# A four-layer decoder on one core: keys and values of two cross attentions behind the expert tiles, expert rows fetched back block by block, VectorE kept in the order of the step table

## Chip, cores and metric

The kernel runs on one core of a Trainium2 chip. The metric is device time in microseconds (us) of one launch. Runs of one kernel differ by some tenths of a per cent, so a time is the median of several.

## What is computed

The input `x` is 32 sequences of 64 tokens with 128 features, and `ctx` is of the same shape. Four layers follow each other, and each has three parts, each with a residual and a layer norm behind it:

```
for each layer:   x = LN(x + attn(x));  x = LN(x + xattn(x, ctx));  x = LN(x + ffn(x))
layer 0: rope attention (16 heads of 8) | gated two-way cross attention | two local-window transformer layers
layer 1: latent attention (16 heads of 64) | cross attention | 8 experts, one per token, none dropped
layer 2: attention with alibi            | cross attention | 8 experts, one per token, at most 80 tokens each
layer 3: rope attention                  | cross attention with masks | linear layer with both sides rounded to fp8
```

What matters here is that the keys and values of a cross attention, `k = ctx Wk + bk` and `v = ctx Wv`, depend on `ctx` alone, and so on nothing that the layers before it compute. In the attention with alibi a number that grows with the distance between query and key is added to each score.

## The kernel before

The 2048 tokens are four blocks (`NBLK`) of 512 tokens, that is eight sequences or four tiles of 128 tokens. `Decoder` has a method for each part of a layer. Each method puts closures into a table, `Steps` (L259): `sp.at(step, place, f)` files `f` under a step and a place within it, and `run` calls all of them in the order of step and place. Steps of different parts interleave, so that one block's attention runs beside the next block's preparation. The order of PE's instructions is that of the table (`manual_schedule` for PE at the end of the program). The order of the other engines' instructions, and of the DMAs issued by SP and POOL, is chosen by a list scheduler when the program is built; each engine then works through its instructions strictly in that order.

An 8-wide attention (`attn8`, L630) has 16 scores, four per block. For block `blk` at base step `base`, `prepare` (L653) runs in three steps the k part, the q part and the v part of `attn8_prep` (L516): a projection on PE, a copy out of PSUM by ACT (for rope, two projections and two DVE operations), and for k the *wide* product `kx` (L561): two tiles of 128x1024, on POOL, where each key row is masked for four heads. `self.wide` is the last of these. The values go into `v8`, two constant tiles that alternate between blocks and hold a column of ones per head. `attn8_scores` (L580) puts masks or alibi into PSUM by bf16 matmuls with an identity, adds q times kx, and then DVE takes the maximum (`mx`, L610) and the difference (`p`), and ACT the exponential (L613). Two steps later `attn8_turn` transposes p on PE (`ptps`, L624) and ACT copies it (`pT`, L626); `values` multiplies with v (`o`). `turn_a`, `out` (y) and `normal_x` finish a half block; `turn_x` (L494) transposes the new x for the next part (`xTps`, `xT`). A norm (`norm`, L458) is bn_stats and bn_aggr on DVE, 1/sqrt by two operations on POOL (`rstd`, L419), and the scaling on ACT, DVE or POOL. Scores have two PSUM buffers, all else on PE shares four (`G`).

Alibi is kept as three bf16 parts. The high and middle parts lie on 128 partitions and go in by one matmul per head group; the low part is on 64 partitions and goes in by a second one.

The experts (`sorted_experts` L1321, `capacity_experts` L1461) work like this: `routed` (L1274) computes logits and choices block by block beside the cross attention and scatters each token's row to a DRAM buffer sorted by expert (POOL, indirect DMA). When all rows are there, tiles of up to 128 rows are loaded, multiplied by their expert's weights, and scattered back to `token_y` in DRAM. The weights of all eight experts lie in `wbig`, 128 partitions by eight times 1156 columns. The first expert stage copies a tile's weights out of `wbig` (L1383); the second reads them in place. `wbig` is refilled for the second by `fetch` (L1468), 24 loads on SP, as soon as the copies of the first are done. Then `rows_back` (L1438 and L1528) loads a block of rows: block 0's behind all scatters, and those of blocks 1 to 3 behind `self.wide` as well, all three from one place in the table. `added` adds the residual (or multiplies by the gate, L1535) and norms; `turn_x` follows. Meanwhile the next attention (l2a in layer 2, l3a in layer 3) starts with block 0.

Names of the parts: l1x, l2x, l3x are the cross attentions of layers 1 to 3, l2a and l3a the self attentions of layers 2 and 3, l1f and l2f the expert stages, l3f the fp8 layer. For l2a the base step is 96, for l2x 112, for l3a 137, for l3x 153.

`fp8_linear` (L1616) rounds the weights once (`weights`: load, ACT product `kh`, then eight DVE operations on `qe` and `em`), and for each block of x rounds it in four DVE pieces, multiplies, adds and norms.

Of the kernel before, what the change touches and what calls it, by code (L numbers as in the profile page):

```python
# [20 lines left out]
P = 128  # L21
# [73 lines left out]
def _alibi():  # L95
# [10 lines left out]
    low = (ali - hi.astype(f) - mid.astype(f)).astype(ml_dtypes.bfloat16)  # L106
    return np.concatenate([np.concatenate([hi, mid], 0), np.concatenate([low, low], 0)], 1)
# [151 lines left out]
class Steps:  # L259


    def __init__(self):
        self.work = {}
# [4 lines left out]
    def run(self):  # L268
        for key in sorted(self.work):
            for f in self.work[key]:  # L270
                f()


class Decoder:
# [66 lines left out]
    def setup(self):  # L341
# [48 lines left out]
        for n in range(2):  # L390
            v = self.const([P, BPB, 8, 2, 9], f"v8_{n}")
            nc.gpsimd.memset(v, 0.0)
            nc.gpsimd.memset(v[0:64, :, :, 0, 8:9], 1.0)
            nc.gpsimd.memset(v[64:128, :, :, 1, 8:9], 1.0)
            self.v8.append(v)

# [30 lines left out]
    def layernorm(self, z, last=False):  # L427
# [3 lines left out]
        for t in range(TPB):  # L431
            nc.vector.bn_stats(st[:, t, :], z[:, t, :])
            nc.vector.bn_aggr(mv[:, t, :], st[:, t, :])
# [24 lines left out]
    def norm(self, blk, z, pool=True, number=False, part=(0, TPB)):  # L458

# [5 lines left out]
        for t in range(n):  # L467
            nc.vector.bn_stats(st[:, t, :], z[:, t0 + t, :])
            nc.vector.bn_aggr(mv[:, t, :], st[:, t, :])  # L469
        r = self.rstd(mv[:, 0:n, 1], n)  # L470
        if t0 == 0:
            full = self.xfull[blk] = self.const([P, TPB, XR], "x", bufs=5)
            self.xt[blk], self.xT[blk] = full[:, :, 0:D], None
            if number:
                nc.gpsimd.tensor_copy(
                    full.bitcast(I32)[:, :, D:], bc(self.tokens[:, blk * TPB : (blk + 1) * TPB], 2, XR - D)
                )
        x = self.xt[blk]
# [15 lines left out]
    def turn_x(self, blk, part=(0, TPB)):  # L494
# [6 lines left out]
        self.nc.scalar.copy(self.xT[blk][:, t0 * P : (t0 + n) * P], ps[:, 0 : n * P])  # L501
# [14 lines left out]
    def attn8_prep(self, blk, w, src, rope, scale, bqs, quick):  # L516
# [23 lines left out]
        def q_part():  # L540
# [3 lines left out]
            elif "bq" in w:  # L544
                nc.scalar.activation(qT, proj("wq", self.xT[blk]), AF.Identity, bias=bqs, scale=scale)
            else:
                nc.scalar.mul(qT, proj("wq", self.xT[blk]), scale)

        def k_part():
            kT = self.q2([P, TB], "k8")  # L550
            if rope is not None:
                turned("wk", "bk", src(blk), rope[:, 128:256], kT)
            elif "bk" in w:
                nc.scalar.activation(kT, proj("wk", src(blk)), AF.Identity, bias=w["bk"], scale=1.0)  # L554
            else:
                nc.scalar.copy(kT, proj("wk", src(blk)))
# [8 lines left out]

        def v_part():
            x = src(blk)
# [5 lines left out]
            v = got["v"] = self.v8[blk % 2]  # L573
# [4 lines left out]
        return got, (k_part, q_part, v_part)  # L578

    def attn8_scores(self, blk, pp, gg, prep, mask):  # L580
# [5 lines left out]
        for h in range(2):  # L586
# [8 lines left out]
            elif kind == "heads":  # L595
                o2 = o.rearrange("p (n c) -> p n c", n=2)
                self.mm(o2, self.ident2, bc(m[:, g * 256 : (g + 1) * 256], 1, 2), True, False)
                self.mm(o2, self.ident2[0:64, :], bc(m[0:64, 1024 + g * 256 : 1024 + (g + 1) * 256], 1, 2), False, False)
# [31 lines left out]
    def attn8(self, sp, base, name, src=None, rope=None, scale=1.0, row=None, mask=(None, None), has_out=True, split=False, number=False, turned=None):  # L630
# [22 lines left out]
        def prepare(blk, i):  # L653
            if i == 0:
                prep[blk] = self.attn8_prep(blk, setup["w"], src, rope, scale, setup.get("bqs"), quick and blk == 0)
            prep[blk][1][i]()
# [80 lines left out]
        sp.at(base - 4, 3, start)  # L737
        for blk in range(NBLK):
            for i in range(3):
                sp.at(base + 4 * blk - 4 + i, 4, lambda blk=blk, i=i: prepare(blk, i))  # L740
# [460 lines left out]
    def route(self, lg, oh, gate=None):  # L1201
# [3 lines left out]
        mx = self.sb([P, TPB], "rmx", 4)[:, 0:n]  # L1205
        nc.vector.tensor_reduce(mx, lg, AX.X, ALU.max)
        if gate is not None:
            self.tt(lg, lg, bc(mx, 2, 8), ALU.subtract)
            nc.scalar.activation(lg, lg, AF.Exp)
# [64 lines left out]
    def routed(self, sp, st, ready, wr, br, base, rows, dst, bound, gated):  # L1274
# [10 lines left out]

        def choose(t0, n):
# [4 lines left out]
            self.route(st.pop(("lg", t0))[:, 0:n, :], st["oh"][:, t, :], st["gate"][:, t] if gated else None)  # L1291
# [479 lines left out]
```

## Time and profile before

| what | value |
|---|---|
| median of 5 runs | 1463.95 us (1458.01 to 1468.05) |
| the profiled execution | 1465.63 us, of which the span from first to last instruction is 1463.9 |
| PE busy | 1242.2 us, 85% of the span |
| DVE, ACT, POOL busy | 925.2, 688.8, 734.8 us |
| mean granted PE clock | 0.882 |
| the chain that ended last | PE 57%, DVE 16%, POOL 12%, ACT 8%, issue 4%, DMA 2% |

The page of the profile lists lines of `kernel.py` (L335 is the helper for all matmuls, L338 the helper for all tensor_tensor operations), so groups are told apart by the names of their tiles: `out<-in`. The windows view cuts the span into stretches that one chooses and gives each engine's busy time in each, the clock that PE was granted (1.00 is full speed), the share of the DMA engines and the GB/s that they moved. The chain of waits goes back from the last instruction, at each step to what released it, and is then listed in order of time: start, length, engine, tile and line. The timeline lists the instructions of an engine in order; for SP these are the DMAs that it issues, with the time at which they were issued. PE's busy time includes half-speed stretches: the same matmul takes longer there.

### The profile page before, as it was taken

The numbers are of one execution on the slowest core, as the hardware profiler recorded it, in microseconds if no ns is written. First come the engines' busy times: TensorE is split into PE (matmuls) and PEld (weight loads), VectorE is DVE, ScalarE is ACT, GpSimd is POOL, SyncE is SP. The second block draws the span as 40 slices with busy tenths as digits, with TensorE's granted clock in tenths as the row PEclk, the third lists the DMA queues.
The fourth block names the chain that finished last, engine by engine and source line by source line (L and its number), as shares of the span: only waits on it lengthen the run. The fifth ranks groups of instructions, "written<-read, shape, count | busy, mean of one in ns | idle before, by whom it ended". The sixth has DMA issues, their size and how long they took to land.

```text
span 1463.9 us, 36933 instructions
## 1 busy us (share of the span) xinstructions
PE 1242.2 (85%) x16009; PEld 898.7 (61%) x16009; DVE 925.2 (63%) x1819; ACT 688.8 (47%) x1174; POOL 734.8 (50%) x609
## 2 busy tenths in 40 slices
PE   7997888889887898989889995949999855899992
PEld 4775555556555555666567775916677753577772
DVE  6754577777786677657564655635677434667775
ACT  3453445555554544554545532634566311546642
POOL 3524688777785655445532443522445232444542
PEclk9998899999999999999999975968999557889955
DMA  6001010350010000100010002230000001000000
GB/s 231 2 2 24 0 45 2 127 163 2 1 53 1 1 1 2 54 14 2 2 34 35 2 17 62 73 118 2 2 9 5 3 12 36 2 1 2 3 9 22
DMA packets 33714, 43.16 MB, mean 29 GB/s; under 512 B 5946, under 2 KB 27121, under 8 KB 33168
## 3 DMA queue, kind: packets, MB, share of 16 engines
q1 hardware_dynamic: 31536, 38.20, 8.1%
q8 instruction: 126, 2.06, 0.6%
q0 software_dynamic: 2016, 2.60, 0.6%
q14 instruction: 36, 0.29, 0.1%
HBM read 26.63 MB, written 15.56 MB: 29 GB/s over the span
## 4 chain that ended last, share of the span: by engine, by line
PE 57%; DVE 16%; POOL 12%; ACT 8%; issue 4%; DMA 2%; SPq 0%; POOLq 0%; ACTq 0%; DVEq 0%
PE s L335 13%; PE o L335 9%; PE ptps L624 6%; PE qkps L335 5%; DVE turn L338 5%; PE proj L335 5%; POOL turn L338 4%; PE y L335 4%; PE ropeT L877 3%; ACT pT L626 2%; DVE rn L1037 2%; POOL rstd L338 2%; DVE p L338 2%; PE vps L335 2%; POOL rn L338 2%
## 5 line engine op out<-in xcount | busy, mean ns | idle before, releaser
L610 DVE TENSOR_REDUCE mx<-s 128x16 f32<-128x1024 f32 x96 | 117.4, 1223 | 133.6 <-PE s L335 132.1
L338 POOL TENSOR_TENSOR turn<-turn,turn 128x1024 f32<-128x1024 f32 x64 | 150.6, 2362 | 92.5 <-DVE turn L338 91.9
L338 DVE TENSOR_TENSOR p<-s,mx 128x1024 f32<-128x1024 f32 (+1 forms) x144 | 158.8, 1103 | 5.2 <-ACT pT L626 0.5
L626 ACT COPY pT<-ptps 128x512 f32<-128x512 f32 x192 | 104.9, 587 | 94.7 <-PE ptps L624 93.3
L335 PEld LDWEIGHTS o<-v,pT 128*64 128x64 f32 x3072 | 111.3, 150 | 47.0 <-ACT pT L626 37.2
L613 ACT ACTIVATE p<-p 128x1024 f32<-128x1024 f32 x96 | 101.4, 1057 | 79.5 <-DVE p L338 78.0
L561 POOL TENSOR_TENSOR kx<-k,w_const 128x1024 f32<-128x1024 f32 x45 | 85.4, 1917 | 101.6 <-ACT k L554 65.9
L335 PE MATMUL o<-v,pT 128*64 128x18 f32 x3072 | 123.2, 221 | 10.5 <-ACT pT L626 8.5
L335 PE MATMUL s<-kx,q 32*64 32x128 f32 x3072 | 118.4, 292 | 6.5 <-DVE sparts L1578 2.5
L624 PE MATMUL ptps<-w_const,p 128*128 128x128 f32 x768 | 118.5, 304 | 0.2 <-ACT c L828 0.2
L335 PEld LDWEIGHTS s<-kx,q 32*64 32x64 f32 x3072 | 91.8, 142 | 43.6 <-issue 40.2
L423 POOL TENSOR_SCALAR rstd<-bnmv 128x4 f32<-128x4 f32 (+1 forms) x60 | 15.2, 254 | 196.4 <-DVE bnmv L469 154.3
L338 DVE TENSOR_TENSOR turn<-qkps,w_const 128x512 f32<-128x512 f32 (+1 forms) x96 | 75.9, 860 | 53.6 <-PE qkps L335 53.6
L624 PEld LDWEIGHTS ptps<-w_const,p 128*128 128x128 f32 x768 | 98.7, 158 | 9.4 <-issue 8.5
L338 POOL TENSOR_TENSOR rn<-rn,nhalf 128x16 f32<-128x16 f32 x32 | 93.6, 2924 | 2.7
L877 PE MATMUL ropeT<-w_const,turn 128*128 128x128 f32 x512 | 69.9, 283 | 23.4 <-ACT oT L935 10.7
L335 PE MATMUL qkps<-wbig,hT 128*128 128x512 f32 x128 | 72.1, 692 | 11.8 <-POOL hT L1013 10.8
L338 DVE TENSOR_TENSOR turn<-qkps,xtab 128x512 f32<-128x512 f32 (+1 forms) x96 | 82.0, 858 | 0.0
L1037 DVE TENSOR_REDUCE rn<-sq 128x16 f32<-128x1024 f32 x32 | 39.0, 1219 | 65.4 <-ACT sq L1033 65.4
L877 PEld LDWEIGHTS ropeT<-w_const,turn 128*128 128x128 f32 x512 | 58.3, 144 | 35.8 <-ACT oT L935 9.9
L483 POOL TENSOR_SCALAR x<-z,bnmv,rstd 128x128 f32<-128x128 f32 x100 | 78.6, 798 | 2.5
L335 PE MATMUL o<-pT,v 64*64 64x64 f32 x2048 | 70.6, 221 | 8.1 <-ACT pT L919 8.1
(333 smaller groups left out, 2729.8 us busy)
## 6 DMA issues: line engine op xcount, KB each, us to landing
sorted_x<-zero SPq DMA_DIRECT2D x9, 990.0 KB
wbig<-in_l1f_w_dram SPq DMA_DIRECT2D x4, 1156.0 KB
wbig<-in_l2f_w_dram SPq DMA_DIRECT2D x16, 256.0 KB
wbig<-in_l0f_dram SPq DMA_DIRECT2D x2, 1561.0 KB
z<-token_y SPq DMA_DIRECT2D x8, 256.0 KB
wbig<-in_l1a_dram SPq DMA_DIRECT2D x1, 1856.0 KB
xsorted<-sorted_x SPq DMA_DIRECT2D x23, 66.0 KB
xT<-in_xT_dram SPq DMA_DIRECT2D x4, 256.0 KB
```

The lines of the kernel that those rows point to most:

```text
L335: self.nc.tensor.matmul(out, lhsT=lhsT, rhs=rhs, start=start, stop=stop)
L338: (eng or self.nc.vector).tensor_tensor(out=out, in0=a, in1=b, op=op)
L423: nc.gpsimd.tensor_scalar(r[:, :n], var, EPS, None, ALU.add)
L483: eng.tensor_scalar(x[:, t0 + t, :], z[:, t0 + t, :], mv[:, t, 0:1], r[:, t : t + 1], ALU.subtract, ALU.mult)
L561: self.wide = eng.tensor_tensor(out=kx, in0=bc(kT, 1, 2), in1=bc(head[:, 2 * i : 2 * i + 2], 2, TB), op=ALU.mult).ins
L610: nc.vector.tensor_reduce(mx, s3, AX.X, ALU.max)
L613: nc.scalar.activation(pr, pr, AF.Exp)
L624: self.nc.tensor.transpose(ps[:, j, :], flat[:, c : c + P], self.ident)
L626: self.nc.scalar.copy(o, ps)
L877: self.nc.tensor.transpose(pt[:, j * P : (j + 1) * P], f[:, j * P : (j + 1) * P], self.ident)
L1037: nc.vector.tensor_reduce(rn, sq, AX.X, ALU.add)
```

## The change

1. `early` is new. For the first blocks of l2x (three) and l3x (four), k and v are computed at step `n - 4`, place 2.6 to 2.8, which is behind the last expert tile and ahead of the turn of block 0's new rows. They are kept in `wbig`, 1152 columns of v and 512 of k per block. The zeros and ones around v are filled there by POOL (even blocks) or DVE (odd blocks), ordered behind `summed`, the last addition of the expert stage. `prepare` then skips these projections.
2. `wbig` is read longer, so `fetch` is cut into three: experts 5 to 7 at the old place, 0 and 1 behind them at the same step, 2 to 4 two steps later.
3. The rows of blocks 1 to 3 come back one by one: block 1's behind the copy of block 0's turn (`turned_at`), blocks 2 and 3 behind the wide product of the block before. Their norms are cut in two: moments in one step, scaling (`ended`) in the next. Their turns are two to six steps apart.
4. In steps 95 to 128 and 136 to 169 the order of DVE is that of the table, too (`fixed`, `keep_order`). Places are moved to suit: k, q and v of l2a's and l3a's later blocks are prepared a step later (`held`), the route is cut into `compare` and `choose`, the fp8 weights into load and rounding two steps later, the fp8 layer's end into `product`, `summed`, `moments`, `ended`.
5. All norms run their four bn_stats first and then their four bn_aggr.
6. The low part of alibi is zero for every second head, so its matmul covers two heads of four, 256 columns in place of 512.

The core of the diff:

```diff
-    def run(self):
-        for key in sorted(self.work):
-            for f in self.work[key]:
-                f()
+    def run(self, keep_order):
+        with ExitStack() as region:
+            inside = False
+            for key in sorted(self.work):
+                if any(a <= key[0] < b for a, b in self.fixed) != inside:
+                    region.close()
+                    inside = not inside
+                    if inside:
+                        region.enter_context(keep_order())
+                for f in self.work[key]:
+                    f()
...
         for t in range(n):
             nc.vector.bn_stats(st[:, t, :], z[:, t0 + t, :])
+        for t in range(n):
             nc.vector.bn_aggr(mv[:, t, :], st[:, t, :])
...
-        self.nc.scalar.copy(self.xT[blk][:, t0 * P : (t0 + n) * P], ps[:, 0 : n * P])
+        self.turned_at = self.nc.scalar.copy(self.xT[blk][:, t0 * P : (t0 + n) * P], ps[:, 0 : n * P]).ins
...
         def k_part():
-            kT = self.q2([P, TB], "k8")
...
+            kT = got.get("kT")
+            if kT is None:
+                kT = self.q2([P, TB], "k8")
+                keys(kT)
...
         def v_part():
+            if "v" not in got:
+                got["v"] = self.v8[blk % 2]
+                values(got["v"])
...
-                self.mm(o2, self.ident2[0:64, :], bc(m[0:64, 1024 + g * 256 : 1024 + (g + 1) * 256], 1, 2), False, False)
+                low = m[0:64, 1024 + g * 256 : 1024 + (g + 1) * 256].rearrange("p (h k) -> p h k", k=S)[:, 0:4:2, :]
+                self.mm(o4[:, :, 0:4:2, :], self.ident2[0:64, :], bc(low, 1, 2), False, False)
...
+        def early(blk, i):
+            n = BPB * 8 * 2 * 9
+            at = blk * (n + TB)
             if i == 0:
+                prep[blk] = self.attn8_prep(blk, self.w[name], src, None, scale, setup, False)
+                v = prep[blk][0]["v"] = self.big[:, at : at + n].rearrange("p (b h u d) -> p b h u d", h=8, u=2, d=9)
+                self.after(self.set_ones(v, nc.vector if blk % 2 else nc.gpsimd), [self.summed])
+                return
+            got, _, keys, values = prep[blk]
+            if i == 1:
+                got["kT"] = self.big[:, at + n : at + n + TB]
+                keys(got["kT"])
+            else:
+                values(got["v"])
...
+        if ahead:
+            step, place, m = ahead
+            for i in range(3):
+                for blk in range(m):
+                    sp.at(step, place + 0.1 * i, lambda blk=blk, i=i: early(blk, i))
...
-                sp.at(base + 4 * blk - 4 + i, 4, lambda blk=blk, i=i: prepare(blk, i))
+                n = base + 4 * blk - 4
+                at = (n + 1 + (i + 1) // 2, 4 + i % 2 / 2) if held and blk else (n + i, 4)
+                sp.at(*at, lambda blk=blk, i=i: prepare(blk, i))
...
-            self.load_after(z[b], self.token_rows(0, b), k["y"] + ([self.wide] if b else []))
+            self.load_after(z[b], self.token_rows(0, b), k["y"] + [[], [self.turned_at], [self.wide], [self.wide]][b])
...
-            self.norm(b, z.pop(b), False if b else "both")
+            if b:
+                k["moments", b] = self.moments(b, z[b])
+            else:
+                self.norm(b, z.pop(b), "both")
+
+        def ended(b):
+            self.normed(b, z.pop(b), k.pop(("moments", b)), False)
...
         sp.at(*prepared, weights)
+        sp.at(step_ + 2, 0.5, kernel)
...
-    back, later = [(n - 4, 3.5), (n, 2), (n + 2, 6), (n + 4, 6)], (n - 1, 2)
-    k.capacity_experts(sp, "l2f", ready, (n - 14, 7), tiles, back, later)
-    k.attn8(sp, n, "l3a", rope=k.c["r3"], row=rows["l3a_bo"], mask=("all", "causal"))
+    back = [
+        (None, (n - 4, 3.5), (n - 4, 3.6)), ((n - 4, 3.7), (n - 1, 5), (n + 1, 2.5)),
+        ((n + 1, 4.5), (n + 3, 6), (n + 5, 3.5)), ((n + 5, 4.5), (n + 7, 6), (n + 9, 3.5)),
+    ]
+    fetched = [(n - 14, 7, (5, 6, 7)), (n - 14, 7.1, (0, 1)), (n - 12, 7, (2, 3, 4))]
+    k.capacity_experts(sp, "l2f", ready, fetched, tiles, back)
+    sp.fixed.append((n - 1, n + 33))
+    k.attn8(sp, n, "l3a", rope=k.c["r3"], row=rows["l3a_bo"], mask=("all", "causal"), held=True)
+    ahead = (n - 4, 2.6, 4)
...
-        sp.run()
+        sp.run(lambda: tc.manual_schedule(engines={mybir.EngineType.DVE}))
```

In `back` each block has three entries: where its rows are loaded, where they are added, and where they are turned. l1f, l2a and l2x are changed alike, with `ahead = (n - 4, 2.6, 3)`.

## The prediction, made before the changed kernel had run

> **What bounds the kernel now.** I read the windows view first, one row per stage from the first expert stage on (before it the instruction order hardly changes). Columns: stretch, its length, busy us (instructions) of PE, PEld, DVE, ACT, POOL, then granted PE clock, DMA share, GB/s.
>
> ```profile
> 952.00:964.00 12.00, 0.09 (x1) 0.09 (x1) 2.58 (x12) 0.63 (x2) 1.76 (x3) 0.58 0.75 245
> 964.00:972.00 8.00, 7.33 (x43) 3.65 (x43) 1.23 (x1) 2.81 (x6) 2.93 (x1) 0.57 0.25 83
> 972.00:980.00 8.00, 1.64 (x34) 0.95 (x33) 5.74 (x16) 1.95 (x3) 1.61 (x2) 0.86 0.26 73
> 980.00:999.00 19.00, 16.84 (x126) 8.77 (x128) 7.14 (x21) 8.71 (x18) 7.49 (x7) 0.52 0.01 1
> 999.00:1070.00 71.00, 70.06 (x1131) 49.57 (x1129) 40.40 (x67) 39.55 (x61) 25.21 (x24) 1.00 0.01 2
> 1070.00:1132.00 62.00, 60.55 (x1177) 50.56 (x1170) 48.58 (x96) 40.93 (x65) 33.93 (x38) 1.00 0.02 7
> ...
> 1218.00:1228.00 10.00, 0.89 (x4) 0.68 (x4) 2.94 (x15) 0.88 (x2) 1.27 (x2) 0.60 0.09 27
> 1228.00:1240.00 12.00, 9.06 (x76) 4.35 (x74) 6.60 (x7) 3.11 (x4) 1.89 (x1) 0.76 0.10 29
> 1240.00:1252.00 12.00, 1.83 (x9) 0.88 (x5) 9.03 (x40) 4.37 (x9) 2.78 (x5) 0.52 0.15 42
> ...
> 1284.00:1303.00 19.00, 16.75 (x192) 13.03 (x192) 9.85 (x22) 7.86 (x12) 5.65 (x7) 0.64 0.01 2
> 1303.00:1378.00 75.00, 73.69 (x1336) 55.48 (x1334) 52.18 (x86) 43.86 (x68) 41.50 (x40) 1.00 0.01 2
> ```
>
> There are two kinds of stage. In the attentions (999 to 1132, 1303 to 1378) PE is busy 98% at full clock and DVE at most 78%: a PE microsecond taken out there is nearly a microsecond of time. Behind each expert stage (952 to 999, 1218 to 1260) PE first stands, then works at half clock. The chain of waits, in order of time, says for what:
>
> ```profile
> 956.36 2.79 DMA z<-token_y
> ...
> 963.91 1.30 PE xTps L498 x4
> 965.24 0.59 ACT xT L501
> 965.88 3.78 PE proj L335 x4
> ...
> 981.36 1.05 POOL rstd L338
> ...
> 983.78 2.07 PE proj L335 x2
> 985.86 3.96 PE s L335 x36
> ```
>
> PE's last expert matmul ends at 951.06; block 0's rows come back by DMA, are normalized and turned at 963.91. After s(0) PE stands again from 973.7 to 980.3, for block 1's rows: SP issues them only behind block 0's wide key product,
>
> ```profile
> 970.02 1.48 SPq L1272 DMA_DIRECT2D z<-token_y  x3
> ```
>
> and DVE mixes their statistics with those of blocks 2 and 3. Then PE runs cold for 18 us (s takes 3.96 us; warm it is 2.2 to 2.3).
>
> **The change, part by part.** Base: the profiled execution, span 1463.9, 1465.6 with what lies around it; the median of the runs is 1463.95, 1.7 below. Everything up to 951 is taken as unchanged.
>
> *Keys and values ahead.* Three k/v pairs of l2x and four of l3x leave the dense stages for the two gaps. A pair is one projection (0.86, chain rows) and one vps set (1.08): 1.94 us, 13.6 for seven. Three of l2x and three of l3x are PE time in dense stages; I count 1.6 each, because vps also covered some waits of o for pT (0.2 to 0.4 us where ptps has nothing behind it). The seventh falls in 1378 to 1398, where DVE is busy 17.4 of 20 us, and counts 0.4. Sum **-10**; ends -13.6 and -4.
>
> What that puts into the gaps: PE 5.8 us (951 to about 957) and 7.8 us (1216.7 to 1224.5), idle before. ACT: per pair one copy of 0.69 and two of 0.63, so 5.9 and 7.8 us; its next work is at 963.37 and 1226.56, so the first has 5 us to spare, the second 1 at most (its v copies wait for POOL's fills, to about 1221). POOL: a fill row is 1.06 us, with its two small ones 1.5; two behind the last scatter (ends 952.5) last to 955.5, rstd is due at 961.2. DVE fills show no row; from nothing to POOL's 1.5 each, in a DVE gap of 7.8 and 5.0 us. All hidden.
>
> The price is `wbig`: experts 0 to 4 (15 loads, 2.8 MB) no longer go out at 950 to 963 but wait on SP until l2x has read its keys. Behind them on SP stand only the three chosen rows, issued at 1192.77. Block 2's last o ended at 1141.7; 1.7 MB at the 245 GB/s of the first row is 7 us; the first expert matmul is at 1196. Cost 0, with 45 us of cover. Fewer loads beside the last scatter help: it landed after 4.65 us against 2.04 behind the second expert stage; I take 1 of these 2.6 us.
>
> *Low part of alibi.* 32 matmuls go from 512 to 256 columns. Four of these bf16 matmuls cost 1.27 us, one 0.32: weight load 0.10, and 0.23 in which the loader waits. Half of the latter, 0.11, times 26 in the dense part: **-2.8** (ends 0 and -4.2).
>
> *Rows block by block, first opening (before: 951 to 999.9, end of o(0)).* z1 waits for block 0's turn (`turned_at`, 965) in place of `wide` (970): it lands near 968, before DVE is through with kx (969.9). add 0.7, statistics 1.2, rstd on POOL 1.35 behind its kx (971.7): ready at 973. nb waits behind mx and p of s(0) on DVE (976), ACT takes exp 1.06 first, then x 1.65: x(1) near 978.5, against 981.8. PE meanwhile does s(1), before the turn now, and stands about 4 us in pieces instead of 6.7 and 1.9. If the clock drops all the same, k 1.0, s(2) 3.6, ptps 1.9, vps and q 3.5, o 1.8 end o(0) near 992, with the scatter's microsecond near 991: **-8.5**; with a full clock near 986 (-14). Lower end 0.
>
> *Second opening (before: 1217 to 1264.5).* PE ends the added work at 1224.5 and turns at 1227.1. z1 is issued at 1229 instead of 1237.5. The chain to s(0) stays DVE's (k, rot, kx 2.47, q): 1 us earlier. x(1) comes near 1245 instead of 1251; the clock drops here once more; o(0) ends near 1257.5: **-7** (ends -2 and -11).
>
> *DVE in the table's order, waits in two.* No work is added or removed. At 1284 DVE let p(s) wait behind the rounding of the fp8 weights (qe, kh); ACT's pT came late, PE stood 2 us, and the clock was half for 13.4 us of full PE work, 6.7 us lost: 8.7 together. The rounding now stands two steps later, with kh ready. Half of it counts, **-4** (0 to -8), since any new stall costs the same. An in-order DVE also adds waits: z adds for blocks 2 and 3 now stand between scores, and behind a late load mx, p, and with them s (two buffers) and PE would queue. z2 is issued behind block 1's kx, a step and a half before its add, so I count no single wait; **+3** for new stalls with their cold stretches (0 to +10). Tail (1398 to the end) and routing: 0, plus or minus 4. Statistics first, then aggregates: the same 1.2 us per four.
>
> Sum -10 - 2.8 - 8.5 - 7 - 4 + 3 = -29.3: span 1434.6, some 1436 for a profiled execution, 1435 for a median.
>
> **A rule against it.** How long PE may stand, by the rows: the clock fell 2.8 us after PE stopped at 951.06 (mean 0.96 in 952 to 954), 4.1 after 973.7, 3.4 after 1216.7. So the first gap, still 6 us, stays cold; the second, 2.6 us, may not. The Trainium skill (TensorE: Matmul & The Clock Gate, Why this matters for your kernels) puts the limit at about 3 us idle, which agrees. The same page (Part 4: PE-mode transpose) says that transposes do not count as busy for the gate in the same way: this change takes projections out and leaves transposes, and by that rule l2x would fall to half clock, which is the slow rival's sum below. The rows speak for a warm l2x: from 1122.7 to 1131.5 it ran without a projection or vps and stayed at 1.00, and fell only at 1134.8, after four PE stalls (1.3 us) at the first scatter.
>
> **Rivals.**
> - *Wide gain*, 1418: the clock survives the openings (-14, -11) and 1284 is clean (-8), nothing lost: -46. For it: the second gap is under 2.8 us. Against: x(1) still comes 3 us after s(1).
> - *Narrow gain*, 1449: openings give little, since rstd, exp and xT stand in line whoever issues z1; -10, -2.8 and some 2 remain.
> - *Even*, 1463: l2x alone goes cold early, +28 as below, and eats everything.
> - *Slower*, 1485: thinned cross attentions lose the clock. A cold l2x step is 6.9 us (1141.7 to 1148.6), the warm one 3.8: +3.1. From block 1 to the drop that is there anyway 9 steps, +28; in l3x 6.9 against 4.2, 8 steps, +22. With the gains +21. It decides from some 10 cold steps more than now. For it: once cold, PE was fully busy from 1136 to 1148 and not released.
>
> **How the numbers follow.** Forecast 0.50, wide 0.20, narrow 0.15, even 0.07, slower 0.08. A measurement tells 0.5%, 7 us, from no change. Faster 0.85, same 0.07, slower 0.08. The range leaves out the last two and some of the ends: 1413 to 1456.
>
> **What would show it.** Right: ctx projections at 951 to 957 and 1217 to 1225; four z loads issued one by one; PE's stand before xTps(1) under 3 us; an l2x block of about 16 us instead of 17.6; s with alibi 2.1; no half clock near 1284. Wrong: clock under 1.00 between the openings and the first scatter; DVE waiting for z loads with PE idle; hps waiting for `wbig`.

## The result and the profile after

The changed kernel takes 1467.5 us (median of 31 runs, 1461.33 to 1472.63) against 1462.51 of the kernel before in the same series: ratio 1.0038, 95% interval 1.0025 to 1.0052. The forecast was 1435; the time lies above its range. The profiled execution takes 1466.72 us, its span is 1464.7 (before 1465.63 and 1463.9), PE is busy 1243.0 us at a mean granted clock of 0.89, DVE 935.6.

The total hardly moved, the stages moved a lot. I cut both spans at the same scores, each by the start of DVE's maximum (`mx`): l2a from its first score to its sixth and to its last, l3a from its first to its sixth and its thirteenth, l3x from its ninth to its last. This is the windows view of the changed kernel (stretch, length, busy us of PE, PEld, DVE, ACT, POOL, granted PE clock, DMA share, GB/s):

```profile
974.30:1005.20 30.90, 27.53 (x347) 17.73 (x347) 15.05 (x26) 14.57 (x24) 7.50 (x7) 0.78 0.03 10
1005.20:1064.40 59.20, 56.69 (x883) 41.69 (x883) 35.32 (x71) 32.70 (x54) 25.86 (x25) 0.97 0.02 6
1227.70:1254.90 27.20, 24.16 (x341) 15.80 (x340) 18.46 (x33) 11.83 (x19) 10.01 (x9) 0.81 0.04 11
1254.90:1313.80 58.90, 49.25 (x629) 35.03 (x630) 37.68 (x80) 23.37 (x41) 26.59 (x25) 0.82 0.02 6
1368.60:1421.30 52.70, 42.53 (x533) 32.24 (x534) 34.28 (x62) 19.72 (x31) 21.56 (x23) 0.65 0.02 6
```

And the same stages of the kernel before:

```profile
973.70:1014.10 40.40, 31.63 (x357) 18.96 (x358) 18.90 (x46) 18.70 (x32) 12.20 (x11) 0.75 0.02 5
1014.10:1070.70 56.60, 55.98 (x908) 39.91 (x909) 33.72 (x57) 30.87 (x48) 22.82 (x24) 1.00 0.01 2
1241.70:1277.30 35.60, 26.71 (x353) 17.27 (x354) 23.64 (x59) 16.71 (x29) 13.50 (x13) 0.78 0.01 3
1277.30:1321.80 44.50, 41.93 (x617) 31.40 (x618) 29.02 (x52) 19.15 (x30) 21.67 (x21) 0.85 0.01 2
1379.20:1421.20 42.00, 40.64 (x567) 30.95 (x568) 32.62 (x61) 21.97 (x34) 15.94 (x17) 0.72 0.03 8
```

Both openings (first and third row) became shorter by 9.5 and 8.4 us, as forecast. What follows them became longer: the rest of l2a by 2.6, the rest of l3a by 14.4, the last half of l3x by 10.7. In the fourth row PE stands for 9.7 us instead of 2.6, in the fifth for 10.2 instead of 1.4. The early keys and values are where they should be, on PE in the gap behind the expert tiles (timeline of PE, changed kernel):

```profile
952.49 2.74 PE L343 MATMUL proj<-ctxT,w_l2x 128*128 128x512 f32 x6
955.16 3.02 PE L343 MATMUL vps<-w_l2x,ctxT 128*64 128x64 f32 x96
```

The chain of waits through l3a names what stands in the fourth row. The step from the sixth score to the seventh takes 11.3 us (before 5.4), and the turn (`ptps`) of the seventh score comes 21.6 us behind that of the fifth (before 16.5). The expectations below take these two turns for one step, and compare them with 5.6.

```profile
1262.82 1.61 DVE sparts L346
...
1264.79 1.50 DVE sparts L346
1266.29 1.15 DVE mx L642
...
1268.68 0.34 DVE z L346
...
1269.07 3.38 PE proj L343 x4
...
1277.72 1.07 ACT p L645
...
1278.80 0.59 ACT pT L658
...
1279.44 1.96 PE o L343 x32
```

`sparts` are the scale parts of the fp8 kernel: nine DVE operations on one column, which the table puts ahead of the maximum of a score that PE had finished at 1262.93. Behind the maximum stand p and z, and z releases the PSUM that the next projection waits for: PE stands 3.37 us and comes back at half clock for some 3 us (3.38 us for four matmuls, 1.98 warm). Then it stands 3.35 us more, since ACT has the exponential of the next score ahead of the copies of pT.

In the fifth row ACT's order shows the same thing (timeline of ACT, changed kernel):

```profile
1373.84 0.58 ACT L658 COPY pT<-ptps 128x512 f32<-128x512 f32 x1
1375.86 1.06 ACT L645 ACTIVATE p<-p 128x1024 f32<-128x1024 f32 x1 [1.44 <-DVE p L346]
1376.83 0.57 ACT L658 COPY pT<-ptps 128x512 f32<-128x512 f32 x1
```

An exponential that waits for DVE stands between the two halves of one pT, and PE pays for it (timeline of PE, changed kernel):

```profile
1377.44 1.27 PE L343 MATMUL o<-wbig,pT 128*64 128x18 f32 x24 [2.00 <-ACT pT L658]
```

### The profile page after: what moved, and what is told of

Read it like the earlier page. It is cut to its first block, busy times and chain, and to the rows that moved or that the text cites. A ratio compares the mean times of both kernels' runs of the same rounds, so it can differ in the third digit from the quotient of the medians.

```text
span 1464.7 us, 36981 instructions
## 1 busy us (share of the span) xinstructions
PE 1243.0 (85%) x16009; PEld 901.3 (62%) x16009; DVE 935.6 (64%) x1828; ACT 688.4 (47%) x1174; POOL 740.9 (51%) x621
## 4 chain that ended last, share of the span: by engine, by line
PE 52%; DVE 18%; POOL 13%; ACT 9%; issue 5%; DMA 2%; another core or an unknown queue 0%; POOLq 0%; SPq 0%; ACTq 0%; DVEq 0%
PE s L343 11%; PE o L343 9%; PE qkps L343 5%; PE ptps L656 5%; PE proj L343 5%; DVE turn L346 5%; POOL turn L346 4%; PE y L343 3%; PE ropeT L933 3%; DVE p L346 2%; ACT pT L658 2%; DVE rn L1093 2%; POOL rn L346 2%; POOL rstd L346 2%; POOL token_y L1319 1%
## 5 line engine op out<-in xcount | busy, mean ns | idle before, releaser
L343 PEld LDWEIGHTS s<-kx,q 32*64 32x64 f32 x3072 | 90.9, 141 | 41.0 <-issue 35.5
L656 PEld LDWEIGHTS ptps<-w_const,p 128*128 128x128 f32 x768 | 98.6, 158 | 9.5 <-issue 8.7
L343 PEld LDWEIGHTS o<-v,pT 128*64 128x64 f32 x2176 | 75.1, 144 | 35.3 <-ACT pT L658 18.8
L580 POOL TENSOR_TENSOR kx<-k,w_const 128x1024 f32<-128x1024 f32 x31 | 59.1, 1926 | 69.2 <-ACT k L589 33.4
L343 PE MATMUL o<-v,pT 128*64 128x18 f32 x2176 | 83.5, 217 | 8.5 <-ACT pT L658 7.4
L343 PE MATMUL o<-pT,v 64*64 64x64 f32 x2048 | 72.3, 224 | 10.2 <-ACT pT L975 10.2
```

The lines of the kernel that those rows point to most:

```text
L343: self.nc.tensor.matmul(out, lhsT=lhsT, rhs=rhs, start=start, stop=stop)
L580: self.wide = eng.tensor_tensor(out=kx, in0=bc(kT, 1, 2), in1=bc(head[:, 2 * i : 2 * i + 2], 2, TB), op=ALU.mult).ins
L656: self.nc.tensor.transpose(ps[:, j, :], flat[:, c : c + P], self.ident)
```

## Experiments

**Theory (order):** the gains are real and are given back where DVE, held to the table, has fp8 work ahead of a score. **Rival (clock):** cross attentions without projections lose the full clock. **Rival (place):** the fp8 work costs among the scores, however DVE is ordered. The kernel before ran at 1446.9 to 1449.0 us on the chips of e1 to e15 and at 1460.5 on that of e16 and e17, so kernels are compared by their ratio to it. The stage times are from each run's profile, cut as above (l2a: first to last score; l3a: first to thirteenth; l3x: ninth to last); these stages agree to 0.1 us between the two profiles of the kernel before. Other kernels agree less: eleven profiles in which DVE has the same order in l2a give 85.3 to 90.2 us for it, and e7 and e11, with the same order of DVE in the last half of l3x, 46.5 and 40.5. So a stage time counts here where several kernels repeat it, and the ratio decides.

| kernel | ratio, 95% interval | l2a | l3a | l3x |
|---|---|---|---|---|
| before | 1 | 97.0 | 80.0 | 42.0 |
| changed | 1.0038 (1.0025 to 1.0052) | 90.1 | 86.0 | 52.7 |
| e1_free | 1.0047 (1.0022 to 1.0072) | 95.9 | 84.9 | 40.5 |
| e2_first | 0.9965 (0.9944 to 0.9986) | 88.5 | 89.1 | 40.5 |
| e4_second | 1.0128 (1.0093 to 1.0164) | 95.8 | 85.0 | 54.7 |
| e3_noahead | 1.0100 (1.0065 to 1.0134) | 89.0 | 91.0 | 46.6 |
| e6_earlylow | 0.9916 (0.9888 to 0.9943) | 89.3 | 80.1 | 37.4 |
| e7_rows | 0.9887 (0.9852 to 0.9923) | 98.6 | 71.6 | 46.5 |
| e8_ordered | 0.9865 (0.9833 to 0.9898) | 87.3 | 77.8 | 40.5 |
| e9_moved | 0.9931 (0.9907 to 0.9955) | 87.3 | 73.9 | 52.9 |
| e10_short | 0.9956 (0.9936 to 0.9975) | 90.2 | 87.3 | 40.5 |
| e11_rows2 | 0.9872 (0.9843 to 0.9901) | 87.3 | 71.3 | 40.5 |
| e12_joined | 0.9856 (0.9829 to 0.9882) | 85.3 | 71.5 | 37.4 |
| e13_parts | 1.0013 (0.9985 to 1.0040) | 90.2 | 86.8 | 52.8 |
| e14_quiet | 1.0027 (1.0000 to 1.0054) | 90.2 | 83.9 | 50.3 |
| e15_quietshort | 0.9934 (0.9910 to 0.9957) | 87.2 | 83.7 | 40.5 |
| e16_kin | 0.9959 (0.9935 to 0.9984) | 87.2 | 77.7 | 50.3 |
| e17_both | 0.9819 (0.9788 to 0.9850) | 87.4 | 73.8 | 37.3 |

### The order on VectorE: e1, e2, e4

All three take out one or both of the two lines

```diff
-    sp.fixed.append((n - 1, n + 33))
```

> The changed kernel with VectorE free of the table's order in both stretches; everything else stays. Theory (order): the changed kernel is 16 us ahead at the fourth score of l3a and loses it twice where VectorE may not pass a piece that another score is behind: 21.6 us for the step to the sixth score of l3a (5.6 before), and some 11 us in the fp8 part (five steps of 7.0 to 11.0, 4.5 to 7 before). Free of the order, these come back less the 3 to 5 us that a free VectorE costs in small stalls: 1440 to 1450. Rival (clock): the losses come from cross attentions without their projections, whose TensorE falls to half clock: the time stays at 1460 to 1468, and l3x is cold from about 1378 as now. Rival (place): the weights and the rounding of the fp8 kernel stand among the scores of l3a whichever way VectorE is ordered: the long step stays over 15 us and the time over 1455.

> The changed kernel with the table's order on VectorE in the first stretch alone (l2a and l2x); from l3a on VectorE is free. Order: both losses lie in the second stretch, the gain of 13 us up to l3a in the first: 1435 to 1446, as e1_free or up to 5 us better. Clock: 1460 to 1468. Place: over 1455.

> The changed kernel with the table's order on VectorE in the second stretch alone (l3a and l3x). Order: both losses stay: 1462 to 1472, within 5 us of the changed kernel. Clock or place: the same, 1460 to 1472; this run tells only whether the order in l2a and l2x gains (slower than the changed kernel) or loses (faster).

The ranges in microseconds were set by the slower chip. On its scale (ratio times 1463.95) e1 comes to 1471 us and e2 to 1459: neither is in the range of "order", both are over the 1455 of "place", and in both one step of l3a stays over 15 us, the eighth score 16.4 and 16.3 us behind the seventh. e4 is 0.9 points slower than the changed kernel, not level with it. The order in the first stretch gains 0.8 to 0.9 points (e2 against e1, changed against e4), in the second it loses 0.7 to 0.8. What no theory had: without any order the change is no better than with it, so something else in it costs a point. e1 shows one place (a second one, in l3a, stands under e11). Its step to the eighth score of l2a takes 13.2 us. On POOL the scaling of the second block's rows stands ahead of `rstd` of the attention's own norm (timeline of POOL, e1):

```profile
1010.96 3.14 POOL L505 TENSOR_SCALAR x<-z,bnmv,rstd 128x128 f32<-128x128 f32 x4
1014.06 0.23 POOL L436 TENSOR_SCALAR rstd<-bnmv 128x4 f32<-128x4 f32 x1
```

and the scheduler has put DVE's small `nb`, which needs it, ahead of a maximum (timeline of DVE, e1):

```profile
1015.45 0.16 DVE L510 SCALAR_TENSOR_TENSOR nb<-bnmv,rstd 128x4 f32<-128x4 f32 x1 [6.31 <-POOL rstd L346]
```

### Early keys alone: e3, and e5 for the chip

```diff
-    k.attn8(sp, n + 16, "l2x", c, ..., number=True, ahead=ahead)
+    k.attn8(sp, n + 16, "l2x", c, ..., number=True)
-    ..., turned=turned, ahead=ahead
+    ..., turned=turned
```

> The changed kernel with keys and values of the two cross attentions back at their places among the scores, as in the kernel before; the rest of the change stays. Order: the early pairs had gained some 5 to 10 us, which go: 1472 to 1480. Clock: TensorE has its projections back in l2x and l3x and stays at full clock: 1450 to 1460. Place: 1467 to 1477.

0.62 points slower than the changed kernel, 9 us (the two intervals leave 0.1 to 1.1 points): the clock rival falls. The early pairs gain, as forecast.

> The kernel before itself once more, with a profile on the chip of these runs, since its earlier profile comes from a chip whose runs were about 1 percent longer. All theories: ratio 1.00; the span at 1440 to 1455.

Span 1451.8. Against the earlier profile 7.8 us are missing between the routing and the tiles of the first expert stage and 9.7 between the twelfth score of l2x and the second; l2a, l3a and l3x are the same. So differences of this size at those two places say nothing about the change.

### Parts of the change without the order: e6, e7

e6 is e7 with, besides, bn_stats and bn_aggr alternating, the route uncut, the eight experts fetched at one place, and the fp8 layer's parts back together (rounding behind the load, sum behind the product). Since experts 2 to 4 are fetched two steps earlier, they land on values that the last scores of l2x still read, so its numbers differ there; instructions and shapes are the same. e7 is e1 with

```diff
-        ((n - 4, 3.7), (n - 1, 5), (n + 1, 2.5)),
-        ((n + 1, 4.5), (n + 3, 6), (n + 5, 3.5)), ((n + 5, 4.5), (n + 7, 6), (n + 9, 3.5)),
+        ((n - 1, 2), (n, 2), (n, 2.1)),
+        ((n - 1, 2.01), (n + 2, 6), (n + 2, 6.1)), ((n - 1, 2.02), (n + 4, 6), (n + 4, 6.1)),
```

in both stretches, norms in one piece, and `held` off.

> The kernel before with two parts of the change alone: the keys and values of seven blocks behind the expert tiles, and the half of the low alibi part. VectorE free, rows back as before, fp8 pieces and routing as before. In e3_noahead against the changed kernel the early pairs were worth 0.6 percent, and 26 pairs of the alibi matmuls at 0.11 us are 2.8 us: theory (order and rows back lose, the rest gains): ratio 0.990 to 0.995. Rival (clock): cross attentions without projections lose the full clock: 1.00 to 1.01.

> e1_free with the rows back and the keys and queries of l2a and l3a at the places of before (rows of three blocks loaded together behind the wide tile, the norm of each right behind its sum). Theory (rows): in e1_free the seventh and eighth score of l2a take 13.2 and 8.0 us, since VectorE's small step of the attention's norm waits 6.3 us for POOL, which has the second block's norm from the rows ahead of it, and in l3a the fourth and eighth 11.1 and 16.4; at the old places these some 15 to 20 us are gone, but the opening takes its 8 us again each time: ratio 0.995 to 1.002 against 1.0047 of e1_free. Rival (fp8 pieces or routing cost): ratio 1.004 to 1.01, no better than e1_free.

Early keys and halved alibi alone are worth 0.84 points, 12 us (0.57 to 1.12 by the interval): the forecast's first two terms (12.8) were right. e7 is 1.6 points better than e1, and better than its theory allowed: rows block by block without the order cost 23 us. e7 also does what I had hoped for at 1284: the eighth to tenth score of l3a take 5.3, 4.2 and 6.5 us, against 9.2, 7.0 and 8.1 in e6.

The reason is not the one I had given, that the rounding stands in front. Though the table has it two steps later in e7, its last operation ends 5.4 us behind the start of the seventh maximum there, 5.1 in e6 and 5.1 in the kernel before. What differs is ACT. In the kernel before, and in e6, an exponential that waits for DVE stands ahead of the copies of pT, and PE stands for them (timelines of ACT and of PE, before):

```profile
1285.35 1.06 ACT L613 ACTIVATE p<-p 128x1024 f32<-128x1024 f32 x1 [1.94 <-DVE p L338]
1286.79 1.05 ACT L626 COPY pT<-ptps 128x512 f32<-128x512 f32 x2
```

```profile
1287.41 1.60 PE L335 MATMUL o<-v,pT 128*64 128x18 f32 x32 [2.01 <-ACT pT L626]
```

In e7 the copies come first, and PE does not stand there (timeline of ACT, e7):

```profile
1263.38 1.08 ACT L658 COPY pT<-ptps 128x512 f32<-128x512 f32 x2
1265.25 1.06 ACT L645 ACTIVATE p<-p 128x1024 f32<-128x1024 f32 x1 [0.80 <-DVE p L346]
```

e7 differs from e6 in several parts; which of them turned ACT's order round is not shown.

### The fp8 work and the order: e8, e9, e10

e9 is the first of these two edits on the changed kernel, e10 the second, e8 both. The first one puts the load (`fetched`), the scale parts and the rounding ahead of the second stretch.

```diff
-    turned = k.fp8_linear(sp, n + 16 + 9, (n + 5, 5.7))
+    turned = k.fp8_linear(sp, n + 16 + 9, (n - 5, 8.2))
...
-        sp.at(step_ + 2, 0.5, kernel)
+        sp.at(step_, 7.9, fetched)
+        sp.at(step_, place + 0.01, kernel)
```

```diff
-    sp.fixed.append((n - 1, n + 33))
+    sp.fixed.append((n - 1, n + 24))
```

> The changed kernel with two edits in the second stretch: the scale parts and the rounding of the fp8 kernel stand ahead of the stretch, beside the routing, and the table's order on VectorE ends with the last score that precedes the fp8 pieces of l3x. If the order is harmless but for the fp8 work that it puts ahead of scores: the step of 21.6 us goes to 6 to 10, the tail is that of e2_first, ratio 0.982 to 0.992, below e2_first (0.9965). If the order itself costs in l3a (VectorE stands for a late operand while a score is ready): 0.996 to 1.004.

> The changed kernel with one edit of e8_ordered alone: the scale parts and the rounding of the fp8 kernel ahead of the second stretch; the order on VectorE holds to the end of l3x, fp8 pieces included. Theory (two prices): the rounding among the scores of l3a costs some 8 to 12 us (step of 21.6 and the cold steps behind it), the fp8 pieces in the order some 10 (the last 16 scores took 88.3 us, 79.9 in the kernel before, 76.1 in e2_first and e8_ordered): ratio 0.992 to 0.998, with the l3x scores still at 84 to 90 us. Rival (one price, the rounding is all): 0.985 to 0.990. Rival (the order in the fp8 part is all): 1.000 to 1.005.

> The changed kernel with the other edit of e8_ordered alone: the order on VectorE ends ahead of the fp8 pieces of l3x; the fp8 kernel is rounded among the scores of l3a. Two prices: the l3x scores at 74 to 80 us, the long step in l3a still over 18: ratio 0.993 to 0.999. Rounding is all: 1.000 to 1.005. Order in the fp8 part is all: 0.985 to 0.990.

Two prices, and within the intervals they add: 1.07 points (15 us) for the fp8 kernel's parts, load and rounding among the scores of l3a, 0.82 (12 us) for the fp8 pieces in the order; both 1.73 (25 us). The seven steps of l3a behind the sixth score take 58.9 us in the changed kernel and 46.6 in e9, at 0.96 of full clock (windows, e9):

```profile
1238.10:1284.70 46.60, 42.14 (x629) 29.94 (x629) 31.41 (x62) 22.83 (x40) 26.21 (x25) 0.96 0.03 7
```

In e10 the last half of l3x takes 40.5 us, as in e1, e2, e8, e11 and e15, where DVE is free there as well. At the score where the changed kernel splits pT (behind `qh`), ACT has both halves together and ahead of the exponential, though DVE has as many operations in the stretch (63, and 62 in the changed kernel; timeline of ACT, e10):

```profile
1367.30 0.68 ACT L534 ACTIVATE qh<-xTps,sparts 128x512 bf16<-128x512 f32 x1
1367.91 1.07 ACT L658 COPY pT<-ptps 128x512 f32<-128x512 f32 x2
1371.79 1.06 ACT L645 ACTIVATE p<-p 128x1024 f32<-128x1024 f32 x1 [1.89 <-DVE p L346]
```

So the order on DVE also changes the order that the list scheduler gives to ACT.

### Rows in the second stretch, and a first sum: e11, e12

e11 is e2 with e7's rows and `held` off in the second stretch alone. e12 adds e9's edit and puts the fp8 pieces back as they were:

```diff
-                (4 * b, 4, [..., (s + 3, 4.5), (s + 4, 0.5), (s + 4, 5.2), (s + 5, 0.5)])
+                (4 * b, 4, [..., (s + 3, 4.5), (s + 3, 4.51), (s + 4, 5.2), (s + 4, 5.21)])
-        pieces.append((8, 4, [...] + [(s, 5.6), (s, 5.7), (s + 1, 3.3), (s + 1, 3.31)]))
+        pieces.append((8, 4, [...] + [(s, 5.6), (s, 5.61), (s + 1, 3.3), (s + 1, 3.31)]))
```

> e2_first (order in the first stretch alone) with the rows back, keys and queries of l3a at the places of the kernel before; the first stretch keeps the rows of one block at a time. Theory (rows): with VectorE free the rows of one block at a time cost in l3a what they cost in e1_free: the steps of 10.1 and 16.3 us go to 5 and 5 to 9, the opening takes its 13 to 16 us for the second score again: from the first expert tile of the stretch to the first score of l3x 128 to 134 us against 148.7, ratio 0.982 to 0.990. Rival (the early rows gain in l3a too): 0.997 to 1.005.

> What the runs so far point to, joined: the first stretch of the changed kernel (rows of one block at a time, VectorE in the table's order), the second of e11_rows2, the fp8 kernel rounded ahead of the stretch, and the fp8 pieces of l3x as in the kernel before; early keys and values and the halved alibi part stay. If the prices add: e8_ordered (0.9865) less 5 us in l3a and 3 in the last scores: ratio 0.979 to 0.984. If they do not: 0.985 to 0.990.

e11 is 0.93 points better than e2. A part of this, whose share is not measured, is when the fp8 weights land. In e2 SP issues their load at 1260.83, behind the rows of the last block; ACT's product `kh` waits for it with pT behind, and PE stands 3.42 us (timeline of ACT, e2):

```profile
1263.56 0.40 ACT L1719 ACTIVATE kh<-kin,sparts 128x128 bf16<-128x128 bf16 x1 [2.91 <-DMA kin<-in_l3f_k_dram]
1263.87 1.05 ACT L658 COPY pT<-ptps 128x512 f32<-128x512 f32 x2
```

Behind it DVE's `nb` waits 3.76 us for POOL ahead of a maximum, as in l2a of e1. With the rows as before, in e11, SP issues the load at 1218.35, nothing waits for it, and the step of 16.3 us takes 5.3. e1 has the same wait (2.86).

e12 misses the 0.979 to 0.984 that it should have had if the prices add. e11 is not measurably better than e7 (0.9872, 0.9887), nor e12 than e17, which differs from it in the second stretch alone (0.9856, 0.9819): whether rows come block by block under the order, or as before with DVE free, makes no difference that these runs can tell, in the first stretch or in the second. The rival (place) falls too: e7 and e11 have the fp8 weights and their rounding among the scores of l3a, as the changed kernel has them, and with DVE free and the rows as before l3a takes 71.3 to 71.6 us. The opening's gain comes back out of the steps behind it. PE's work there tells why, as far as l2a goes. In e6, rows as before, the second row of l2a reads

```profile
1007.50:1060.30 52.80, 52.17 (x874) 38.86 (x875) 33.72 (x57) 29.06 (x45) 22.07 (x22) 1.00 0.01 2
```

and in the changed kernel, with the same matmuls in all, 59.20 and 56.69 busy, partly at half clock (0.97). e8 has the same first stretch and ran this row at full clock (windows, e8):

```profile
1000.90:1058.60 57.70, 55.19 (x883) 40.31 (x883) 35.18 (x71) 32.63 (x54) 25.87 (x25) 1.00 0.02 7
```

So 3.0 us of turns and projections of blocks 2 and 3 (eight `xTps`, two `proj`), which PE did at the opening, are now done where it has next to no free time, and PE stands 2.5 us there in place of 0.6. Of the 6.9 us that the opening gains (29.6 in e8, 36.5 in e6) 4.9 come back. In l3a all of it does: from e12 to e17 the opening goes from 35.3 to 27.2 us and the seven steps behind the sixth score from 36.2 to 46.6, with PE 42.2 us busy in place of 35.5.

### What in the fp8 kernel costs: e13, e14, e15, e16, e17

e13 moves the scale parts alone ahead of the stretch, e14 only two DVE operations forward, to a place where POOL rests, e15 is e14 with e10's edit. e16 is e13 with the load ahead as well. e17 is e8 with e12's pieces.

```diff
+        sp.at(step_ - 10, 8.2, scales)
```

```diff
+        sp.at(step_, 3.9, scales)
```

```diff
-            kin = self.q2([P, D], "kin", BF16)
-            self.load(kin, self.ins["l3f_k"])
+            kin = k["kin"] = k["q"]
...
+        sp.at(step_ - 10, 7.9, scales)
```

> The changed kernel with the scale parts alone (nine tiny DVE operations on one column) ahead of the second stretch; the weights' load, their product on ACT and the rounding stay where they are, and so does the whole order. In the changed kernel two of these, each 0.14 to 0.16 us when DVE does them early (151 and 159 in the kernel before), take 1.61 and 1.50 us and end 0.03 us behind the two kx products of POOL, 1264.40 and 1266.27. Theory (blocked parts): they are what begins the long step; without them score, p, z and the projection come 4 us earlier, PE stands under 1 us there and may stay at full clock: the step of 21.6 goes to 6 to 12 and the ratio to 0.992 to 0.998, near e9_moved (0.9931). Rival (rounding): the eight operations on qe two steps later are the price: ratio 1.001 to 1.005, the long step over 15.

> The changed kernel with the same scale parts moved by two DVE operations only: ahead of k and rot of the third block in place of behind a, in a stretch in which POOL has no work (idle from 1253.3 to 1261.2) and DVE waits 2.07 us for a projection; the order holds, nothing else moves. Theory (blocked parts, by POOL): the two subtractions take 0.14 to 0.2 us each in place of 1.61 and 1.50, the nine together 1.2 to 1.6 us inside DVE's wait, and the time is that of e13_parts within 0.3 percent: 0.992 to 0.999. Rival (any DVE work there costs, or the subtractions are slow by themselves, in a cold row of the table): they stay over 1 us and the ratio over 1.000.

> e14_quiet with the order on VectorE ended ahead of the fp8 pieces of l3x (the edit of e10_short). If the prices add, blocked parts 0.5 to 1.1 points and the order in the fp8 part 0.8: ratio 0.984 to 0.992, near e8_ordered (0.9865). If the rounding among the scores is a price of its own: 0.992 to 0.997.

> e13_parts with the fp8 weights loaded ahead of the second stretch as well (into the tile that their rounded form takes later), so that ACT's product kh has no DMA to wait for; the product and the eight operations on qe stay among the scores of l3a. In e13_parts kh stood 2.74 us for the load, with the copies of pT behind it on ACT, and PE 3.25 us for pT; 9 us later PE stood 2.48 us more, since ACT has the exponential of the next score ahead of pT. Theory (load on the way): with the first stand gone PE enters the next score warm, and most of what e9_moved gains (1.07 points) is there: ratio 0.991 to 0.996. Rival (order of ACT): the second stand comes all the same and drops the clock: 0.997 to 1.000. Rival (rounding on DVE): 1.000 to 1.004.

> e8_ordered with the fp8 pieces of l3x at the places of the kernel before, as in e12_joined, where the last eight scores took 37.4 us against 40.5. If that adds: ratio 0.982 to 0.987 (e8_ordered 0.9865). If it does not: 0.987 to 0.990.

"Blocked parts" is right on the operations and wrong on the time. In e14 the two subtractions take 0.16 us each, 1.61 and 1.50 in the changed kernel, where they run beside POOL (timelines of DVE in e14 and of POOL in the changed kernel):

```profile
1242.75 0.16 DVE L346 TENSOR_TENSOR sparts<-w_rows,sparts 128x1 f32<-128x1 f32 x1
```

```profile
1262.53 3.74 POOL L580 TENSOR_TENSOR kx<-k,w_const 128x1024 f32<-128x1024 f32 x2
```

Yet without them the time falls by a tenth (e14) or a quarter of a point (e13), inside the intervals. e15 is 0.2 points better than e10, not the 0.5 to 1.1 that "blocked parts" gave. The next wait took their place: in e13 ACT's product `kh` waits for its weights, and pT is behind it on ACT (timeline of ACT, then of PE, e13):

```profile
1261.32 0.40 ACT L1721 ACTIVATE kh<-kin,sparts 128x128 bf16<-128x128 bf16 x1 [2.74 <-DMA kin<-in_l3f_k_dram]
1261.63 1.05 ACT L658 COPY pT<-ptps 128x512 f32<-128x512 f32 x2
```

```profile
1262.24 2.08 PE L343 MATMUL proj<-xT,w_l3a 128*128 128x512 f32 x2 [3.25 <-ACT pT L658]
```

The load is short, but SP issues it behind the rows of the last block, as in e2: in the changed kernel at 1266.75, covered there by the parts. e16 takes that wait away: the seven steps fall from 58.0 to 50.5 us, the ratio by half a point, to 0.9959, the upper end of what its theory gave. What is left to e9's 46.6 is the exponential ahead of pT on ACT, with 3.35 us of standing as in the changed kernel (timeline of PE, e16):

```profile
1270.56 1.90 PE L343 MATMUL o<-v,pT 128*64 128x18 f32 x32 [3.35 <-ACT pT L658]
```

At the same score of e9 ACT copies pT at 1254.05, ahead of the exponential at 1256.02, and PE stands 0.29 us. So three waits lay behind each other; each hid the next. Whether that last stand needs the rounding's eight operations or only the ACT order that comes with them was not separated. e17, the sum of what gained, has the lowest ratio: 1435.42 us, 1.8% below the kernel before and 2.2 points below the changed one; its interval overlaps those of e8 and e12.

## Why the prediction was wrong

Forecast -29.3, measured +0.8 us of span between the two profiles and +5.0 between the medians. By its steps:

- **Keys and values ahead, -10: right in the total.** e3 gives 9 us. The stages show less: the first eleven steps of l2x went from 50.7 to 49.0, the first eight of l3x from 37.9 to 35.6, and two pairs left each, so that is about 1 us a pair where I had counted 1.6. The gaps hide the work, as said (40.5 us from the first `eps`, the second product of the first expert tile of l2f, to the first score of l3a, before 41.4).
- **`wbig` behind l2x, 0: right.** The experts begin no later: the first `eps` comes 44.9 us behind the last score of l2x, before 49.7 and, in e5, 46.3.
- **Low alibi part, -2.8: right.** In the dense part such a matmul fell from 387 to 280 ns; times 26 that is 2.8 us.
- **Slow rival: fell.** From 1068 to 1117 l2x runs at a clock of 1.00 and PE is busy 48.1 of 49 us; e3, with the projections back, is slower.
- **First opening -8.5, second -7: right as stages (-9.5, -8.4), wrong as gains.** The step that failed: I counted an earlier o(0) as time gained and did not ask which PE work the opening had held, though I had written that PE is busy 98% behind it. What is left is none in l3a (73.8 in e17, 71.5 in e12) and 2 us in l2a (87.3 in e8, 89.3 in e6), which is less than profiles of l2a differ by.
- **Hiccup -4: the gain is there without the order, the reading was wrong.** I had p wait behind the rounding; only one `qe` of 0.34 us stands ahead of it. pT came late because ACT had the exponential ahead of it, and 8 us come back where it has not (e7 against e6, 71.6 and 80.1), with the rounding where it was. Under the order the gain is lost, since pieces that a free DVE takes early now stand in a row: in the kernel before the scale parts were done at 10.7 to 16.9 us, at the start of the program.
- **"I count no single wait; +3 for new stalls": the step that failed most.** It measured 25 us (e8 against the changed kernel). I had followed DVE's own row for late loads and found none, but not what the order puts ahead of a score (the parts, the fp8 pieces), nor what stands behind DVE on the scheduler's other engines (ACT's exponential ahead of pT), nor SP, where the load of the fp8 weights queues behind rows that are now fetched one by one.
- **Tail, 0 plus or minus 4: wrong.** 42.0 became 52.7, though with the early pairs it is 37.3 to 37.4 where the order is absent and the pieces stand as before (e6, e12, e17).

Of the signs, the l2x block (16.2 us) and the projections of `ctx` right behind the expert tiles (at 952 and 1203) came as said. "No half clock near 1284" did not (0.82 in the seven steps of l3a). Of the signs of being wrong, a clock under 1.00 between the openings and the first scatter came, but not from thinned cross attentions.

## What to carry to other kernels

A wait that is taken out at the opening of a stage gains only what the engine did not use it for: if PE's work in it moves to a stage without free time, it is paid there. Fixing one engine's order helps where scores and rows compete and costs wherever the table puts side work ahead of a score, and the scheduler's order of the other engines changes with it: read their rows, and the DMA queue's, too. When a removed wait gains nothing, look for the next one that it hid before giving up the theory.

## What the hardware showed

A DVE operation on two tensors of one column took 0.14 to 0.16 us by itself (kernel before, e14) and, in the changed kernel, 1.61 and 1.50 us when it began while POOL was in a product of two tensors: it ended at 1264.43 and 1266.29, just behind POOL's two products, which end at 1264.42 and 1266.27. e10 shows the same pair (1.61 and 1.49). The Trainium skill (SBUF — State Buffer, SBUF: two separate sides) states that the two engines share a pair of ports which one holds for a whole instruction, and the rows agree.

The clock fell after PE had stood for only 2.00 us (to 1377.44), and stayed at half for 21 us in which PE was busy all but 0.4 (windows, changed kernel):

```profile
1378.00:1399.00 21.00, 20.64 (x240) 15.87 (x238) 14.46 (x24) 6.21 (x9) 7.69 (x9) 0.52 0.01 2
```

e9 does the same at the same place (stands 2.00 us, then 0.53 from 1348 to 1369), while in e10 stands of 0.56 and 0.77 left it at 1.00. The Trainium skill (TensorE: Matmul & The Clock Gate, What's actually happening and Why this matters for your kernels) puts the limits at about 3 us of idling and 3.4 us of busy time; both rows differ from it, and they decide here. In the kernel before, too, the 32 matmuls of the score behind the stand of 2.01 us (to 1287.41) take 1.98 us, and 1.10 warm.
